# Where the copy of the rotated half into place 4 is written in the row loop of a spectral convolution

## The chip, the core and the metric

The kernel runs on one core of a Trainium2 chip. A core has five engines, each with its own queue of instructions: TensorE (PE in the profile; PEld is its weight load), VectorE (DVE), ScalarE (ACT), GpSimd (POOL) and SyncE (SP), which here only issues DMAs. An engine's sequencer that issues a DMA is shown as SPq or POOLq. The metric is the time of one execution on the device in microseconds (us), the median of the runs shown.

## The reference, cut to what matters

The input is four images of 512 by 512 places with 16 channels, in float32. Two layers follow each other, each added to its input: a convolution with a filter as large as the image, done by Fourier transforms, and a 3 by 3 convolution with a cosine norm. The change lies in the first:

```python
x = x + _L0_conv_ref(_gn(x), h0, numerators, denumerator)
# _L0_conv_ref: the filter is a ratio of two polynomials, H_full in frequency space
X = jnp.fft.rfft2(x, s=(2 * l1, 2 * l2), axes=(-3, -2))
Y = jnp.einsum('...hwi,ijhw->...hwj', X, H_full)
y = jnp.fft.irfft2(Y, s=(2 * l1, 2 * l2), axes=(-3, -2))
return y[..., :l1, :l2, :]
```

`_gn` is a group norm. The einsum mixes the 16 input channels into 16 output channels at every frequency; the changed copy belongs to this step.

## The kernel before, in words

The program has four phases, one after the other: `filter_phase` makes the filter, `forward_phase` transforms the images along their width, `conv_phase` transforms, mixes and transforms back along the height, and `last_phase` finishes the width and does the second layer. The change touches `conv_phase` alone.

`conv_phase` walks over 513 rows. A row is one frequency along the width (the first is done in two planes, which is why there are 513 and not 512). For row n it does the following, spread over five steps of the loop so that several rows are under way at once.

- `load_x` (L697 and on) fetches the row's input and `turn_x` (L708 and on) makes the transform matrix of the row: one ScalarE instruction (tile turn, L718) and one VectorE instruction (L720).
- `x_part` (L723 and on) transforms it with four matrix products into px (L731), and an eviction copies px into **place 0** of the tile xe. The tile xe has eight places; the other seven hold the same spectrum moved by 16 partitions per place, so that `mix` can use them together.
- `x_late` (L738 and on) stores place 0 to the scratch tensor xf_d in device memory (L745). Then GpSimd makes **xl**, place 0 turned by a fixed set of angles, in six instructions: four products into xu (L752), one product into xl (L753) and one sum into xl (L754). Then xl is stored to xf_d as well (L745). The pool of xl has one buffer (`xlp`, one buffer per tile unless another number is given).
- `load_xe` (L766) reads places 1 to 3 and 5 to 7 of xe back from xf_d with two DMAs on SyncE's queue, which move the partitions by their addresses.
- `half_shift` (L760) makes **place 4** without a DMA. Half 0 copies the upper 64 partitions of place 0 into the lower 64 of place 4. Half 1 copies the lower 64 partitions of xl, the rotated half, into the upper 64 of place 4. Both are copies of 64 by 1024 elements on ScalarE (L763). Half 1 is the copy that the change is about.
- `g_part` (L775) expands the row of the filter into gh, `mix` (L792) multiplies xe by gh into pm, and the eviction of pm makes yf. `over_q` (L812) and `over_g` (L842) transform back and store the result to y_d from GpSimd's queue (L868).

Evictions of PSUM go through `evict` (L678 and on): every third is done by VectorE (L681), the others by ScalarE (L683). In nearly every row ScalarE so has 17 instructions: four evictions into yf, four into gh, four copies into zq (L827), one eviction into yo, one into xe, one turn and the two copies of `half_shift`.

What sets the order: `step(n)` (L876) runs for n from -3 to 514 and writes the work in four quarters, k = 0 to 3. Each quarter has a quarter of `mix` of row n, of `g_part` of row n + 1 and of `over_q` of row n - 1. Quarter 0 has also `x_part` and `x_late` of row n + 2, quarter 2 has `turn_x` of row n + 3 and `over_g` of row n - 2. In the kernel before, quarter 2 has half 0 and quarter 3 has half 1 of `half_shift` of row n + 2. No engine's queue is written out by hand: a scheduler takes the instructions in the order of the source as priorities, places each on its engine's queue, and adds the waits that data and buffers demand. Once the program is built, each engine runs its queue in its fixed order.

Of the kernel before, what the change touches and what calls it, by code (L numbers as in the profile page):

```python
# [46 lines left out]
P = 128  # L47
# [153 lines left out]
def bc(ap, axis, shape):  # L201
    return ap.unsqueeze(axis).to_broadcast(shape)
# [447 lines left out]
def conv_phase(tc, cst, g_d, x_d, y_d):  # L650
    nc = tc.nc
    with ExitStack() as ctx:
# [22 lines left out]
        state = {}  # L675
# [9 lines left out]
        def load_g(n):  # L685
            rc, r, plane = rows[n]
            g = io.tile([P, C, 8 * C], F32, name="g")
            t, w = g.rearrange("p j x -> p (j x)"), C * 8 * C
            if plane is None:
                nc.sync.dma_start(out=t, in_=dram(g_d[rc], r, 0, [w, P], [1, w]))  # L690
            else:
                for to, at in ((0, (0, 96)[plane]), (64, (64, 32)[plane])):
                    nc.sync.dma_start(out=t[to : to + 32], in_=dram(g_d[rc], r, at * w, [w, 32], [1, w]))
                    nc.gpsimd.memset(t[to + 32 : to + 64], 0.0)
            state["g", n] = g

        def load_x(n):  # L697
            rc, r, plane = rows[n]
            x = io.tile([P, B, 8 * C], F32, name="x")
            t, w = x.rearrange("p b x -> p (b x)"), B * 8 * C  # L700
            if plane is None:
                nc.sync.dma_start(out=t, in_=dram(x_d[rc], r, 0, [w, P], [1, w]))
            else:
                nc.gpsimd.memset(t[S:], 0.0)
                nc.sync.dma_start(out=t[:S], in_=dram(x_d[rc], r, plane * S * w, [w, S], [1, w]))
            state["x", n] = x

        def turn_x(n):  # L708

            for k in range(2) if n == 0 else [n // 64 + 1] if n % 64 == 0 else []:  # L710
                if k < 9:
                    state["own", k] = xlp.tile([P, 2, 64], F32, name="own", bufs=3)
                    nc.sync.dma_start(
                        out=state["own", k].rearrange("p v n -> p (v n)"), in_=cst["own"][:, 128 * k : 128 * k + 128]
                    )
            own, at = state["own", n // 64], slice(n % 64, n % 64 + 1)
            t = xlp.tile([P, 2 * F], F32, name="turn")
            nc.scalar.activation(t, dfs[:, 1], AF.Identity, scale=own[:, 1, at])  # L718
            m = xlp.tile([P, 2 * F], F32, name="dfs_n", bufs=2)
            nc.vector.scalar_tensor_tensor(m, dfs[:, 0], own[:, 0, at], t, ALU.mult, ALU.add)  # L720
            state["dfs", n] = m

        def x_part(n, b):  # L723

            if b == 0:

                state["xe", n] = xep.tile([P, 8, F, 2, 2, 2], F32, name="xe")
            if b % 2 == 0:
                state["px"] = ps_f.tile([P, 2, F, 2], F32, name="px", tag="full")
            px = state["px"]  # L730
            nc.tensor.matmul(px[:, b % 2].rearrange("p f c -> p (f c)"), state["x", n][:, b],  # L731
                             state["dfs", n], start=True, stop=True)
            if b % 2:
                evict(state["xe", n][:, 0, :, b // 2], px.rearrange("p k f c -> p f c k"))
            if b == B - 1:
                del state["x", n], state["dfs", n]

        def x_late(n):  # L738

            xe = state["xe", n][:, 0]  # L740
            fl = xe.rearrange("p f h c k -> p f (h c k)")

            def store(half, t):
                at = slice(C, P) if half == 0 else slice(0, P - C)
                nc.gpsimd.dma_start(out=xf_d[n % 4][half * P :, :][at], in_=t[at].rearrange("p f x -> p (f x)"))  # L745

            store(0, fl)
            xl = xlp.tile([P, F, 2, 2, 2], F32, name="xl")
            u = xlp.tile([P, F, 2, 2, 2], F32, name="xu")
            for c in range(2):  # L750
                for h in range(2):
                    nc.gpsimd.tensor_mul(u[:, :, h, c], xe[:, :, h, 1 - c], bc(late[:, 1 + c], 2, [P, F, 2]))  # L752
            nc.gpsimd.tensor_mul(xl.rearrange("p f h c k -> p f (h c k)"), fl, bc(late[:, 0], 2, [P, F, 8]))  # L753
            nc.gpsimd.tensor_add(xl.rearrange("p f h c k -> p (f h c k)"),  # L754
                                 xl.rearrange("p f h c k -> p (f h c k)"),
                                 u.rearrange("p f h c k -> p (f h c k)"))
            store(1, xl.rearrange("p f h c k -> p f (h c k)"))
            state["xl"] = xl

        def half_shift(n, half):  # L760

            dst, src = ((slice(0, 64), state["xe", n][64:, 0]), (slice(64, P), state["xl"][:64]))[half]
            nc.scalar.copy(state["xe", n][dst, 4].rearrange("p f h c k -> p (f h c k)"),  # L763
                           src.rearrange("p f h c k -> p (f h c k)"))

        def load_xe(n):  # L766
            src = xf_d[n % 4]
            for t in (1, 5):
                nc.sync.dma_start(
                    out=state["xe", n][:, t : t + 3].rearrange("p t f h c k -> p t (f h c k)"),  # L770
                    in_=bass.AP(tensor=src.tensor, offset=src.offset + t * C * XF,
                                ap=[[XF, P], [C * XF, 3], [1, XF]]),
                )

        def g_part(n, j):  # L775


            if j % 4 == 0:
                state["pg"] = [ps_g.tile([P, 4, F], F32, name=f"pg{c}", tag="pg") for c in range(2)]
            g, pg = state["g", n], state["pg"]  # L780
            for c in range(2):
                half = slice(64 * c, 64 * c + 64)
                nc.tensor.matmul(pg[c][:, j % 4], g[half, j], dg[half], start=True, stop=True)  # L783
            if j == 3:
                state["gh", n] = ghp.tile([P, F, 2, C], F32, name="gh")
            if j % 4 == 3:
                for c in range(2):
                    evict(state["gh", n][:, :, c, j - 3 : j + 1], pg[c].rearrange("p j f -> p f j"))
            if j == C - 1:
                del state["g", n]  # L790

        def mix(n, g):  # L792

            if g % 8 == 0:
                state["pm"] = ps_m.tile([P, 8, 8, 2 * B], F32, name="pm")
            xe, gh, pm = state["xe", n], state["gh", n], state["pm"]
            for q in range(4):
                f = g + 32 * q
                nc.tensor.matmul(  # L799
                    pm[32 * q : 32 * q + 32, g % 8], gh[:, f].rearrange("p c j -> p (c j)"),  # L800
                    xe[:, :, f].rearrange("p t h c k -> p t (h c k)"), start=True, stop=True,
                )
            if g == 7:

                state["y", n] = yp.tile([P, 16, 32, 4], F32, name="yf")
            if g % 8 == 7:
                evict(state["y", n][:, :, g - 7 : g + 1].rearrange("p t g x -> p g t x"),
                      pm.rearrange("p g t (h x) -> p g (t h) x", h=2))
            if g == 31:
                del state["xe", n], state["gh", n]  # L810
# [65 lines left out]
        def step(n):  # L876


            def row(k):
                return 0 <= n + k < n_rows  # L880

            if row(3):
                load_x(n + 3)
            if row(2):
                load_g(n + 2)
            if row(1):
                load_xe(n + 1)
            for k in range(4):
                if row(0):
                    for g in range(8):  # L890
                        mix(n, 8 * k + g)
                if row(1):
                    for j in range(4):
                        g_part(n + 1, 4 * k + j)
                if row(-1):
                    for t in range(4):
                        over_q(n - 1, 4 * k + t)
                if row(2) and k == 0:
                    for m in range(B):
                        x_part(n + 2, m)  # L900
                    x_late(n + 2)
                if row(2) and k >= 2:
                    half_shift(n + 2, k - 2)
                if row(3) and k == 2:
                    turn_x(n + 3)
                if row(-2) and k == 2:
                    for m in range(4):
                        over_g(n - 2, m)

        for n in range(-3, n_rows + 2):  # L910
            step(n)
# [443 lines left out]
```

## Time and profile before

| what | us |
|---|---|
| median of 3 runs | 19007.57 |
| lowest and highest run | 19006.79 and 19023.34 |
| the profiled execution, its own time | 19054.31 |
| its span, first to last instruction | 19052.5 |
| PE busy, DVE busy, ACT busy, POOL busy in the span | 17293.1, 11398.8, 9747.4, 11564.3 |

Instructions of L763 start between 6958.5 us and 16013.2 us of the span, which marks the stretch of `conv_phase`. Over 512 rows, 6966 to 16013 us, a row takes 9047 / 512 = 17.67 us.

How to read a line of the timeline: start, duration, engine, source line, operation, the tile written and the tile read with their sizes, how many instructions are merged, and in brackets how long the engine was idle before it and whose end ended that wait. In a list of waits, the line that waited stands left of the arrow, the line that released it right, then the total, the count and the longest.

### The profile page before, as it was taken

The numbers are of one execution on the slowest core, as the hardware profiler recorded it, in microseconds if no ns is written. First come the engines' busy times: TensorE is split into PE (matmuls) and PEld (weight loads), VectorE is DVE, ScalarE is ACT, GpSimd is POOL, SyncE is SP. The second block draws the span as 40 slices with busy tenths as digits, with TensorE's granted clock in tenths as the row PEclk, the third lists the DMA queues.
The fourth block names the chain that finished last, engine by engine and source line by source line (L and its number), as shares of the span: only waits on it lengthen the run. The fifth ranks groups of instructions, "written<-read, shape, count | busy, mean of one in ns | idle before, by whom it ended". The sixth has DMA issues, their size and how long they took to land. (4 is left out here: it accounts for less than half of the span.)

```text
span 19052.5 us, 536690 instructions
## 1 busy us (share of the span) xinstructions
PE 17293.1 (91%) x227020; PEld 12605.2 (66%) x227020; DVE 11398.8 (60%) x23961; ACT 9747.4 (51%) x17871; POOL 11564.3 (61%) x12445
## 2 busy tenths in 40 slices
PE   8899999999999988898888888888888888979999
PEld 5455555555554457777777777777777776868888
DVE  8877777777763335555555555555555554347656
ACT  4455555555552235555555555555555553107777
POOL 7577777777771126666666666666666664127655
PEclk7899999999999999999999999999999999999999
DMA  3755455555557668888888888888888887796321
GB/s 100 206 153 148 137 150 150 146 139 149 149 151 223 187 211 320 323 322 324 320 322 317 322 327 317 322 324 323 320 325 323 321 320 282 268 321 210 131 72 62
DMA packets 2918658, 4543.39 MB, mean 238 GB/s; under 512 B 117442, under 2 KB 2086300, under 8 KB 2809374
## 3 DMA queue, kind: packets, MB, share of 16 engines
q1 hardware_dynamic: 2686062, 3768.91, 58.5%
q0 software_dynamic: 174896, 605.89, 8.3%
q10 hardware_dynamic: 55296, 134.24, 2.1%
q8 instruction: 1789, 29.31, 0.6%
q14 instruction: 615, 5.04, 0.1%
HBM read 3031.23 MB, written 1477.31 MB: 237 GB/s over the span
## 5 line engine op out<-in xcount | busy, mean ns | idle before, releaser
L783 PE MATMUL pg<-c_dg,g 64*128 64x128 f32 x32832 | 2842.9, 291 | 320.9 <-ACT gh L683 159.5
L799 PE MATMUL pm<-xe,gh 128*32 128x64 f32 x131328 | 2403.4, 222 | 576.2 <-issue 353.1
L799 PEld LDWEIGHTS pm<-xe,gh 128*32 128x32 f32 x131328 | 2012.8, 110 | 1180.2 <-issue 996.4
L783 PEld LDWEIGHTS pg<-c_dg,g 64*128 64x128 f32 x32832 | 2283.2, 190 | 662.7 <-issue 262.5
L372 PE MATMUL pg<-c_dinv,sp 128*128 128x256 f32 x8192 | 2278.4, 426 | 294.3 <-ACT st L377 193.8
L828 DVE TENSOR_TENSOR z<-zq,pz 128x256 f32<-128x256 f32 x2052 | 862.0, 420 | 2617.2 <-ACT zq L827 2534.6
L348 DVE RECIPROCAL dn<-dn 128x256 f32<-128x256 f32 x1024 | 1790.8, 1749 | 778.3 <-POOL dn L341 778.0
L372 PEld LDWEIGHTS pg<-c_dinv,sp 128*128 128x128 f32 x8192 | 1609.9, 207 | 946.8 <-ACT st L377 215.3
L681 DVE COPY gh<-pg 128x512 f32<-128x512 f32 x2046 | 1410.5, 689 | 1294.1 <-PE pg L783 1289.6
L417 PE MATMUL pt<-ev_in,c_todd 128*128 128x512 f32 x4096 | 1970.1, 606 | 45.6 <-DMA ev_in<-g_d 27.0
L752 POOL TENSOR_TENSOR xu<-xe,c_late 128x256 f32<-128x256 f32 x2052 | 1393.4, 705 | 856.3 <-ACT xe L683 832.3
L335 ACT COPY ab<-pab 128x512 f32<-128x512 f32 x2048 | 1104.2, 592 | 1130.1 <-POOL m L355 333.3
L683 ACT COPY yf<-pm 128x512 f32<-128x512 f32 x2046 | 1210.5, 592 | 919.0 <-PE pm L799 904.3
L377 ACT COPY st<-pg 128x256 f32<-128x256 f32 x2048 | 1072.6, 623 | 1024.0 <-PE pg L372 619.3
L763 ACT COPY xe<-xl 64x1024 f32<-64x1024 f32 x513 | 538.8, 1050 | 1877.0 <-POOL xl L754 1877.0
L350 POOL TENSOR_TENSOR x<-ab,ab 128x256 f32<-128x256 f32 x1024 | 875.8, 855 | 933.6 <-ACT ab L335 907.0
L1208 PE MATMUL pc<-l_band,xn 128*128 128x160 f32 (+3 forms) x9024 | 1374.8, 309 | 65.0 <-DVE e_o L1255 64.0
L683 ACT COPY gh<-pg 128x512 f32<-128x512 f32 x2058 | 1201.2, 584 | 402.0 <-PE pg L783 393.6
L820 PE MATMUL pz<-c_ident,yf 128*128 128x128 f32 x8208 | 1378.2, 291 | 27.2 <-issue 25.4
L1208 PEld LDWEIGHTS pc<-l_band,xn 128*128 128x128 f32 x9024 | 1218.8, 197 | 224.7 <-issue 147.2
L329 PEld LDWEIGHTS pab<-c_e,u 18*128 18x128 f32 x8192 | 723.5, 188 | 809.5 <-ACT st L377 452.5
L417 PEld LDWEIGHTS pt<-ev_in,c_todd 128*128 128x128 f32 x4096 | 806.8, 198 | 669.9 <-issue 514.6
(195 smaller groups left out, 33846.4 us busy)
## 6 DMA issues: line engine op xcount, KB each, us to landing
xe<-xf_d SPq DMA_DIRECT2D x1026, 1536.0 KB, 10.3
g<-g_d SPq DMA_DIRECT2D x511, 1024.0 KB, 9.9
g_d<-st SPq DMA_DIRECT2D x64, 4096.0 KB, 34.3
ev_in<-g_d SPq DMA_DIRECT2D x1024, 256.0 KB, 4.8
g_d<-ot SPq DMA_DIRECT2D x1024, 256.0 KB, 2.9
xf_d<-xe POOLq DMA_DIRECT2D x513, 448.0 KB, 8.3
xf_d<-xl POOLq DMA_DIRECT2D x513, 448.0 KB, 5.3
x_d<-xo SPq DMA_DIRECT2D x128, 1024.0 KB, 5.1
```

What stands on the lines that cost most here:

```text
L335: nc.scalar.copy(w["ab"][n], pp[n])
L348: nc.vector.reciprocal(w["dn"], w["dn"])
L372: nc.tensor.matmul(pg[:, k].rearrange("p a x -> p (a x)"), w["sp"][:, k, c, :], dinv[:, 2 * kp + k, c, :], start=(c == 0), stop=(c == 1),)
L377: nc.scalar.copy(st[a][:, :, i].rearrange("p (q k x) -> p k q x", q=2, k=4)[:, 2 * kp : 2 * kp + 2], pg[:, :, a].rearrange("p k (q x) -> p ...
L417: nc.tensor.matmul(pt, todd[:, c, kc, hh * P : hh * P + P], ev[:, kc, c], start=(kc == 0), stop=(kc == 1),)
L681: nc.vector.tensor_copy(dst, src)
L683: nc.scalar.copy(dst, src)
L752: nc.gpsimd.tensor_mul(u[:, :, h, c], xe[:, :, h, 1 - c], bc(late[:, 1 + c], 2, [P, F, 2]))
L783: nc.tensor.matmul(pg[c][:, j % 4], g[half, j], dg[half], start=True, stop=True)
L799: nc.tensor.matmul(pm[32 * q : 32 * q + 32, g % 8], gh[:, f].rearrange("p c j -> p (c j)"), xe[:, :, f].rearrange("p t h c k -> p t (h c k ...
L820: nc.tensor.transpose(pz[:, t % 4].rearrange("p v q x -> p (v q x)"), y[:, at].rearrange("p g x -> p (g x)"), ident)
L1208: nc.tensor.matmul(pc[:, lo:hi, :].rearrange("p w j -> p (w j)"), xns[q][:, h * P + dh : h * P + dh + P], bands[dh][:, o : o + hi - lo, :] ...
```

## The change

Half 1 of `half_shift` is written in quarter 1 of the next step instead of quarter 3 of its own step. It still works on the same row: `half_shift(n + 1, 1)` in step n copies what `x_late` made in step n - 1. As another row's xl has been made in quarter 0 in between, xl is kept in `state` by its row. Half 0 stays in quarter 2.

```diff
             store(1, xl.rearrange("p f h c k -> p f (h c k)"))
-            state["xl"] = xl
+            state["xl", n] = xl
...
-            dst, src = ((slice(0, 64), state["xe", n][64:, 0]), (slice(64, P), state["xl"][:64]))[half]
+            dst, src = ((slice(0, 64), state["xe", n][64:, 0]), (slice(64, P), state["xl", n][:64]))[half]
...
-                if row(2) and k >= 2:
-                    half_shift(n + 2, k - 2)
+                if row(1) and k == 1:
+                    half_shift(n + 1, 1)
+                    del state["xl", n + 1]
+                if row(2) and k == 2:
+                    half_shift(n + 2, 0)
```

## The prediction

> **What bounds the kernel now.** I read the page first: busy shares, then the 40 slices, then the costliest groups. PE is busy for 91% of the span, and in the slices of the row stage its digit is 8 or 9 throughout, while ACT shows 5 and POOL 6. So PE sets the pace of the rows, and ScalarE matters only where PE waits for it. The chain of waits that ended last lies in the last phase and does not bear on the change. The waits of PE in the stretch of the rows, 6966 to 16013 us, say where PE loses time:
>
> ```profile
> PE pm L799 <- issue: 349.6, 355, 3.2
> PE pg L783 <- ACT gh L683: 159.1, 177, 5.4
> PE pg L783 <- issue: 156.6, 111, 3.4
> PE pm L799 <- DMA xe<-xf_d: 73.7, 51, 3.0
> PE pm L799 <- ACT zq L827: 62.3, 172, 0.4
> ```
>
> PE's idle time there, all lines of that list added, is 950 us of 9047. ScalarE's share of it is 159.1 + 62.3 = 221.4 us. The next view is the same list for ScalarE. Its largest wait is the one that the change speaks of:
>
> ```profile
> ACT xe L763 <- POOL xl L754: 1872.7, 512, 6.5
> ```
>
> Once in every row ScalarE stands for 1872.7 / 512 = 3.66 us until GpSimd has the rotated half ready. The timeline of ScalarE shows what stands where in one row:
>
> ```profile
> 10008.87 0.59 ACT L683 COPY xe<-px 128x512 f32<-128x512 f32 x1 [0.45 <-PE px L731]
> 10010.81 1.05 ACT L763 COPY xe<-xe 64x1024 f32<-64x1024 f32 x1 [1.35 <-DVE xe L681]
> 10011.76 0.58 ACT L683 COPY yf<-pm 128x512 f32<-128x512 f32 x1
> 10012.36 0.52 ACT L718 ACTIVATE turn<-c_dfs,own 128x256 f32<-128x256 f32 x1
> 10012.78 0.57 ACT L683 COPY gh<-pg 128x512 f32<-128x512 f32 x1
> 10013.25 0.38 ACT L827 COPY zq<-pz 128x256 f32<-128x256 f32 x1
> 10017.33 1.06 ACT L763 COPY xe<-xl 64x1024 f32<-64x1024 f32 x1 [3.70 <-POOL xl L754]
> 10018.41 0.59 ACT L683 COPY yf<-pm 128x512 f32<-128x512 f32 x1
> ```
>
> The reader is to see two things. The copy of half 1 stands fourth after the copy of half 0, behind the first zq that follows it, and that is quarter 1 of the step. The source before writes half 0 in quarter 2 and half 1 in quarter 3. So the queue is not the order of the source: **the scheduler had already brought both copies (and turn, which the source writes in quarter 2) forward**, to where their inputs are due by its own reckoning. GpSimd's timeline in the same row and the next gives the other end:
>
> ```profile
> 10012.89 1.97 POOL L753 TENSOR_TENSOR xl<-xe,c_late 128x1024 f32<-128x1024 f32 x1
> 10014.94 2.36 POOL L754 TENSOR_TENSOR xl<-xl,xu 128x1024 f32<-128x1024 f32 x1
> 10017.59 0.57 POOL L745 DMA_DIRECT2D xf_d<-xl  x1 [0.29 <-POOL xl L754]
> ...
> 10030.06 1.98 POOL L753 TENSOR_TENSOR xl<-xe,c_late 128x1024 f32<-128x1024 f32 x1
> ```
>
> xl has one buffer. The copy can run between the end of L754 (10017.30) and the next row's L753 (10030.06), which overwrites xl. Any queue that holds the data right must put it in that gap of 12.8 us or hold L753 back.
>
> **The change, part by part.** It adds and removes no instruction: 513 copies of half 1, mean 1049 ns, before and after, the same two store DMAs, the same waits for data. What could change is the place of one instruction in ScalarE's queue, and with it what waits behind it. Whether it changes is a matter of the built programs, because the scheduler, not the source, makes the queues. I laid the two programs' queues beside each other, instruction by instruction. One row of ScalarE's queue, the same places in both (buffer numbers as built, before left of the bar):
>
> ```
> 10017 xe<-px  xe_106040<-px_106041 | xe_106039<-px_106040
> 10018 half 0  xe_106040<-xe_106040 | xe_106039<-xe_106039
> 10019 yf      yf_106012<-pm_106059 | yf_106011<-pm_106058
> 10020 turn                         | the same
> 10021 gh      gh_106024<-pg_106093 | gh_106023<-pg_106092
> 10022 zq      zq_106110<-pz_106105 | zq_106109<-pz_106104
> 10023 half 1  xe_106040<-xl_106050 | xe_106039<-xl_106049
> ```
>
> In both, half 1 copies the xl of the row whose place 0 was evicted six instructions earlier. The buffer numbers are smaller by one because the source makes its names one copy earlier; the row is the same. The source now writes the copy half a step later, and the scheduler brings it forward by that much more, to the same place. Over the whole program the queues have the same lengths (ScalarE 24,789 entries with its pure waits, GpSimd 16,634, VectorE 27,854, TensorE 122,696, SyncE 9,324), and place by place the same operations, shapes, buffer addresses and waits with the same counts. What differs is names and line numbers.
>
> So the sum is: instructions added 0, removed 0, moved 0; DMAs moved on SyncE's or GpSimd's queue 0; the stall of 3.66 us in each row stays; **change 0 us**. The profiled execution, 19054.31 us with a span of 19052.5, lies 46.7 us above the median of the three runs; a sum of zero on it is a sum of zero on the median, and the forecast is the median, 19007.57 us.
>
> The Trainium skill has a rule that such a stall invites: "Perfetto Trace Analysis", section Optimization Strategy, says that a gap that repeats on the engine that ought to be saturated can come from too few buffers for the next tile. The row against it: in the rows' stretch GpSimd never waits for the copy before it overwrites the single xl (its L753 waited 3.1 us in all, and for a DMA), and the engine with the gap is not the saturated one. By the rule a later copy would need a second buffer before it could pay; by the row the buffer is not what holds ScalarE. Neither moves the sum, as no instruction moves.
>
> **The rivals.**
>
> 1. *The move does reach the queue and frees ScalarE (faster).* This is what the words of the change say. Then the 3.66 us stall goes and the evictions behind it come on time. Speaking for it: the stall is in 512 rows, and in the row after the one shown PE stood 1.10 us for an eviction of gh just after it. Against it: the two queues above. What it would give: nothing, where the yf and gh evictions are early enough; at most all of PE's idle time, 950 us; I take ScalarE's part of PE's waits, 221.4 us, since the other releasers are not ScalarE's: 19007.57 - 221.4 = 18786 us.
>
> 2. *The move reaches the queue and holds GpSimd back (slower).* With one buffer of xl, the next row's L753 must wait for the copy. In the next row zq of quarter 1 begins at 10030.39 and takes 0.38, the copy 1.05 behind it would end at 10031.82, and L753, which began at 10030.06, would begin 1.76 us late. The sum L754 and the store behind it on GpSimd's queue come as late, then the loads of xe on SyncE's queue, and mix at the end. It decides from the point where the loads of xe are what PE waits for, which they are already in 51 rows (73.7 us). GpSimd itself idles enough to hide it (2.38 us before its next store to y_d in that row). If none is absorbed, 512 x 1.76 = 901 us: 19909 us. If all is, 0. Against it again the queues.
>
> 3. *The same program, but its time lies elsewhere than the three runs (either way).* The three runs span 16.5 us, 0.09%. A difference of more than 0.2%, 38 us, which is about what a measurement of this kernel can tell from no change, would be over twice that.
>
> **How the numbers follow.** The forecast, no change, gets 0.96. Rival 1 gets 0.01 and rival 2 gets 0.01, since both need a queue other than the one built. Rival 3 gets 0.02, one half to each side. So faster 0.02, same 0.96, slower 0.02. The time is the median, 19007.57 us. For the range no unknown cost is left, only the scatter of the runs: the lowest run less their whole spread, 19006.79 - 16.5 = 18990, and the highest plus it, 19023.34 + 16.5 = 19040. Cases outside it hold less than 2 in 10.
>
> **What would show it.** In the profile of the changed kernel ScalarE should wait for GpSimd's xl 512 times or so, about 1870 us in all, now under the same line number. The timeline should have half 1 behind turn, gh and zq, and L753 should wait for nothing of ScalarE's. PE's wait for ScalarE's gh should be near 160 us. It would be wrong if the wait for xl were gone or much shorter, if L753 (with its line as it is) waited for the copy, or if the copies of half 1 began a row later than their xl ended. A span that differs by more than 38 us with all these rows alike would speak for rival 3.

## The result, and the profile after

The changed kernel took 19012.21 us, the median of 12 runs from 18977.92 to 19042.25 us. Beside it the kernel before took 19014.25 us, the median of 12 runs from 18987.79 to 19045.35 us. The ratio is 1.0 with a 95% interval from 0.9993 to 1.0008: no difference that can be measured. The profiled execution of after has a span of 19024.1 us against 19052.5 us before, which is within the scatter of the runs.

The rows that the prediction rests on, in the profile after. First PE's waits in the rows' stretch (6966 to 16013 us); the columns are total us, times, longest:

```profile
PE pm L799 <- issue: 312.7, 320, 2.9
PE pg L783 <- ACT gh L683: 182.3, 197, 5.1
PE pg L783 <- issue: 149.5, 102, 3.2
PE pm L799 <- DMA xe<-xf_d: 95.0, 62, 3.0
PE pm L799 <- ACT zq L827: 63.5, 178, 0.4
```

ScalarE's waits in the same stretch:

```profile
ACT xe L763 <- POOL xl L754: 1881.9, 513, 6.5
```

The stall is where it was: 1881.9 us in 513 rows, 3.67 us each, against 1872.7 us in 512 rows before. PE's rows differ by up to 37 us with no change of order, which says how far one profiled execution of this kernel is to be read. ScalarE's timeline in one row, and then GpSimd's:

```profile
10014.84 0.59 ACT L683 COPY xe<-px 128x512 f32<-128x512 f32 x1 [0.45 <-PE px L731]
10016.91 1.04 ACT L763 COPY xe<-xe 64x1024 f32<-64x1024 f32 x1 [1.48 <-DVE xe L681]
10017.86 0.57 ACT L683 COPY yf<-pm 128x512 f32<-128x512 f32 x1
10018.46 0.51 ACT L718 ACTIVATE turn<-c_dfs,own 128x256 f32<-128x256 f32 x1
10018.88 0.57 ACT L683 COPY gh<-pg 128x512 f32<-128x512 f32 x1
10019.45 0.38 ACT L827 COPY zq<-pz 128x256 f32<-128x256 f32 x1
10023.47 1.05 ACT L763 COPY xe<-xl 64x1024 f32<-64x1024 f32 x1 [3.63 <-POOL xl L754]
```

```profile
10021.07 2.36 POOL L754 TENSOR_TENSOR xl<-xl,xu 128x1024 f32<-128x1024 f32 x1
10023.73 0.58 POOL L745 DMA_DIRECT2D xf_d<-xl  x1 [0.29 <-POOL xl L754]
...
10035.90 1.97 POOL L753 TENSOR_TENSOR xl<-xe,c_late 128x1024 f32<-128x1024 f32 x1
```

Half 1 still stands behind yf, turn, gh and zq, the fifth instruction after half 0 (the prediction's "fourth" is a miscount of the same rows); it starts 0.04 us after the sum L754 of its own row has ended (10021.07 + 2.36 = 10023.43), and the next L753 waits for nothing. The copy that the source now writes in the next step runs where it always ran. Over the whole program the two traces have, engine by engine, the same operations on the same tiles in the same order: 17,871 instructions on ScalarE, 12,445 on GpSimd, 23,961 on VectorE. Of TensorE's 227,020 matmuls 8 stand in other places, all of them products into py that change places with a neighbour in the record.

### The profile page after: what moved, and what is told of

Read it like the earlier page. It is cut to its first block, busy times and chain, and to the rows that moved or that the text cites. A ratio compares the mean times of both kernels' runs of the same rounds, so it can differ in the third digit from the quotient of the medians.

```text
span 19024.1 us, 536690 instructions
## 1 busy us (share of the span) xinstructions
PE 17301.1 (91%) x227020; PEld 12607.2 (66%) x227020; DVE 11386.2 (60%) x23961; ACT 9742.6 (51%) x17871; POOL 11567.4 (61%) x12445
## 5 line engine op out<-in xcount | busy, mean ns | idle before, releaser
L763 ACT COPY xe<-xl 64x1024 f32<-64x1024 f32 x513 | 538.6, 1050 | 1881.9 <-POOL xl L754 1881.9
```

## The experiments

The change never reached the queue, so its result says nothing of what the words describe. The experiments make the move real and then ask why it is worth what it is worth. In these kernels `state["zq"]` holds the last zq copy that was written, and `tc.issue_after(ins)` adds an edge of the issue order: what is written under it stands behind `ins` in that engine's queue. It adds no wait for data. "Before" is the kernel before, run beside each group on the same chip. Its median moved between groups (19015.5 to 19071.95 us), so each version is given as a ratio to the runs of "before" in its own group.

| what | ratio to before, 95% interval |
|---|---|
| half 1 reads place 0: no stall | 1.0008, 0.9999 to 1.0017 |
| half 1 behind quarter 2 | 1.0, 0.9991 to 1.0009 |
| half 1 behind quarter 3 | 1.0004, 0.9995 to 1.0014 |
| half 1 behind quarter 1 of the next step, one xl | 1.0047, 1.0034 to 1.006 |
| the same, two xl | 1.0017, 1.0009 to 1.0026 |
| half 1 behind quarter 3, half of xu on VectorE | 0.9996, 0.9987 to 1.0004 |
| half the filters not loaded, stall kept | 1.0009, 1.0 to 1.0018 |
| half the filters not loaded, half 1 behind quarter 3 | 0.982, 0.9807 to 0.9833 |
| half the filters not loaded, half 1 in the next step | 0.9858, 0.9842 to 0.9875 |
| place 2 by copies on both engines, half 1 behind quarter 3 | 1.1662, 1.1646 to 1.1678 |
| place 2 by copies on both engines, stall kept | 1.1497, 1.1481 to 1.1514 |
| place 2 by copies on ScalarE, half 1 behind quarter 3 | 0.9907, 0.9893 to 0.992 |

**The stall alone.** Half 1 reads place 0, which is ready long before.

```diff
-... (slice(64, P), state["xl"][:64]))[half]
+... (slice(64, P), state["xe", n][:64, 0]))[half]
```

> Half 1 of half_shift reads place 0 (the evicted spectrum) instead of xl, so the upper half of place 4 isn't the rotated half and the product is another; the copy keeps its shape, its length and about its place, but waits for GpSimd no longer. It prices the stall of 3.66 us per row alone. Theory A (the stall costs what PE waits for ScalarE behind it): PE's 159 us for gh and 62 us for zq mostly go, 100 to 220 us faster, 18790 to 18910 us. Theory B (the stall is hidden, because the evictions wait out in PSUM buffers and PE's row is set by its own work and by the loads of xe): within 0.2% of before, under 38 us. Both expect ScalarE's wait for xl at zero.

Measured: 1.0008, so the end of the stall alone wins nothing. Its 3.66 us per row went, and with it PE's waits for ScalarE's gh and zq (zq: 0.7 us; no row for gh); PE's wait for the loads of xe took their place (253.0 us in 128 waits, against 73.7 before):

```profile
PE pm L799 <- DMA xe<-xf_d: 253.0, 128, 4.9
```

The copy was expected to keep about its place and didn't: the two copies now have only a yf between them and stand ahead of turn, gh and zq. Theory B holds for the time. Theory A was right that PE's waits for ScalarE go, and wrong that the time goes with them.

**The move made real, in three steps.**

```diff
-                if row(2) and k >= 2:
-                    half_shift(n + 2, k - 2)
+                if row(2) and k == 2:
+                    half_shift(n + 2, 0)
+                if row(2) and k == 3:        # 2 in the first version
+                    with tc.issue_after(state["zq"]) if "zq" in state else ExitStack():
+                        half_shift(n + 2, 1)
```

In the third version the last two lines stand ahead of half 0, with `row(1) and k == 1` and `half_shift(n + 1, 1)`.

> Half 1 really moves: an edge in the issue order holds it behind the zq copy of quarter 2 of the same step, three instructions later in ScalarE's queue; one buffer of xl. The evictions of yf, gh and zq that stood behind the stall now stand ahead of it. Theory A: the wait for xl falls from 3.66 us per row to 1 us or less and PE's waits for ScalarE fall by more than half, 100 to 200 us faster. Theory B: same within 38 us. A move that harms (the eviction into yo now stands behind the copy, as does the rest) would show as slower by over 38 us.

> As the one before, but half 1 is held behind the zq copy of quarter 3, seven instructions later, about where the source before writes it. Theory A: the wait for xl is gone (xl is ready some 4 us earlier), 100 to 220 us faster. Theory B: same within 38 us. L753 of the next row starts some 9 us later, so it should not wait for the copy under either.

> Half 1 is held behind the zq copy of quarter 1 of the next step, 16 instructions later: what the words of the change say, with one buffer of xl, as the changed source has it. The second rival of the prediction: L753 of the next row waits for the copy, 1.76 us per row late at the timings of before, so GpSimd shows a wait for ScalarE's L763-line copy in nearly every row, and the time is up to 901 us longer if nothing absorbs it. Theory A with GpSimd's idle time absorbing it: 100 to 220 us faster. Theory B: same. I expect the wait to be there and most of it absorbed: between 100 us faster and 200 us slower.

Measured: 1.0, 1.0004 and 1.0047. Behind quarter 3 ScalarE's wait for xl is gone, and the list of PE's waits is another:

```profile
PE pm L799 <- issue: 423.7, 399, 4.3
PE pm L799 <- DMA xe<-xf_d: 295.9, 122, 4.9
PE pg L783 <- issue: 148.7, 117, 3.2
...
PE pg L783 <- ACT gh L683: 11.5, 3, 5.8
```

Against before, the wait for ScalarE's gh fell from 159.1 to 11.5 us and the wait for the loads of xe rose from 73.7 to 295.9 us. What ScalarE gave back, the loads took; the row of mix without a releaser rose as well, from 349.6 to 423.7 us. The granted clock was a little lower, 0.97 against 0.98 between 7000 and 15600 us, but PE's busy time per matmul was 43.9 ns in both (7663.80 us over 174516 matmuls, 7699.59 over 175214 before), so the clock isn't what took the gain. Behind quarter 2 part of ScalarE's wait stays, 543.0 us in 370 waits, and PE's wait for gh is down to 11.0 us all the same.

In the next step, with one buffer of xl, GpSimd's timeline has the wait that the prediction's second rival worked out:

```profile
10014.04 1.97 POOL L753 TENSOR_TENSOR xl<-xe,c_late 128x1024 f32<-128x1024 f32 x1 [1.82 <-ACT xe L763]
10016.09 2.38 POOL L754 TENSOR_TENSOR xl<-xl,xu 128x1024 f32<-128x1024 f32 x1
```

L753 stands 1.82 us for the copy in this row and 907.8 us in all. Yet the kernel lost only 0.47%, some 90 us (0.0047 x 19058). PE's largest wait is now the loads of xe, 428.1 us in 230 waits. My expectation of the wait and of its absorption held; theory A's gain did not come.

**Is L753's wait the cost?** Two buffers of xl; xu moves to place 5 of xe to make room.

```diff
-            xl = xlp.tile([P, F, 2, 2, 2], F32, name="xl")
-            u = xlp.tile([P, F, 2, 2, 2], F32, name="xu")
+            xl = xlp.tile([P, F, 2, 2, 2], F32, name="xl", bufs=2)
+            u = state["xe", n][:, 5]
```

> Half 1 forced to quarter 1 of the next step again, but with two buffers of xl, so that L753 need not wait for the copy; to make room xu is kept in place 5 of the same row's xe, which the load fills only later. If the 0.47% that the one-buffer version lost came from L753's wait (908 us in its profile) through the later store and loads, this one is the same as before within 0.2%, and GpSimd's wait for the copy and the added wait of PE for the loads of xe are gone. If it came from the later copy itself or from something else in that order, it stays 0.3 to 0.6% slower.

Measured: 1.0017. L753's wait is gone here, and the loss is 0.17% instead of 0.47%. The two ratios come from two groups and xu has moved as well, so that L753's wait made up most of the loss is likely and not cleanly shown. The remainder of 0.17% is just clear of zero; whether it is the later copy or the other place of xu wasn't tried apart. One part of the expectation failed: PE's added wait for the loads of xe isn't gone. It is 275.2 us up to 15900 us, near the 295.9 of half 1 behind quarter 3.

**What the loads are worth, with the stall and without.**

```diff
             rc, r, plane = rows[n]
+            if n > 3 and n % 2:
+                state["g", n] = state["g", n - 1]
+                return
             g = io.tile([P, C, 8 * C], F32, name="g")
```

> The kernel before with every second row's filter left out: odd rows reuse the tile g of the row before, so 1024 KB less are loaded in every second row (9% of the 5504 KB that a row moves); the result uses the wrong filter there. The stall of ScalarE stays. Theory C (the rows are paced by how many bytes the DMA engines can move, 0.87 busy at 321 GB/s): PE's waits for the loads of xe go and the time falls, by at most 9% of 9047 = 840 us, by 150 us or more. Theory D (they are paced by the chain from GpSimd's xl through its store to the load, whatever the bytes): less than 80 us. Theory E (PE's own work paces them): within 38 us.

> The same with every second row's filter left out, and with half 1 held behind the zq copy of quarter 3, so without ScalarE's stall. If the stall was worth nothing only because the loads set the pace, it is worth something here: 60 to 220 us faster than the version that leaves out the filter alone. If the stall is hidden by PE's own work too, the two are within 38 us of each other.

> Every second row's filter left out, and half 1 held behind the zq copy of quarter 1 of the next step with one buffer of xl: what the words of the change say, where the loads have room. Theory F: ScalarE's stall is gone and the loads have slack to take up L753's wait of some 1.8 us, 200 to 350 us faster. If L753's wait and the later store cost time even then: within 100 us of before or slower.

Measured: 1.0009, 0.982 and 0.9858. The first two, beside half 1 behind quarter 3 (1.0004), settle the cause. Taking the stall away gives nothing, making the loads lighter gives nothing, and both together give 1.8%. Theory C fails by itself, since the lighter loads alone won nothing. Theories D and E foresaw just that and fail in the second version: it differs from half 1 behind quarter 3 (1.0004) in the loads of the filter alone, neither in GpSimd's instructions nor in PE's, and is 362.5 us faster than the one with the stall (19077.4 to 18714.86 us). That is more than the 60 to 220 us expected. PE's waits with lighter loads and the stall kept (three lines added to the function, so mix is L802 and gh's product L786):

```profile
PE pm L802 <- issue: 539.4, 453, 4.0
PE pg L786 <- issue: 139.4, 105, 4.3
PE pg L786 <- ACT gh L683: 121.6, 136, 5.1
PE pm L802 <- ACT zq L830: 108.2, 293, 0.6
```

The loads of xe are in no row of the list any more; ScalarE's gh and zq are, 229.8 us. The row of mix without a releaser rose from 349.6 to 539.4 us. With the stall gone as well:

```profile
PE pm L802 <- issue: 498.8, 417, 4.3
PE pg L786 <- issue: 155.7, 132, 3.1
...
PE pg L786 <- ACT gh L683: 10.6, 3, 5.1
...
PE pm L802 <- DMA xe<-xf_d: 7.3, 11, 3.1
```

The waits for ScalarE and for the loads are near zero, and only then do the rows come faster. The version in the next step gains 1.4% with lighter loads although L753 still waits (937.4 us up to 15900 us): the move that the words of the change describe would have paid where the loads have room.

**Bytes or the chain to the load?** Two of the four products into xu on VectorE shorten GpSimd's chain.

```diff
-                    nc.gpsimd.tensor_mul(u[:, :, h, c], ...)
+                    (nc.vector if c else nc.gpsimd).tensor_mul(u[:, :, h, c], ...)
```

> Half 1 held behind the zq copy of quarter 3, and two of the four products into xu are made by VectorE instead of GpSimd, so that GpSimd's chain to the rotated half is 1.4 us shorter per row and its store leaves earlier; the bytes are the same. Theory D: PE's wait for the loads of xe (296 us with half 1 in quarter 3) falls by half or more and the time by 100 to 250 us. Theory C: it falls little, the time is within 60 us of before, as VectorE has the time to spare.

Measured: 0.9996, and PE's wait for the loads of xe 276.1 us up to 15900 us, hardly less than the 295.9 up to 16013. The result is not a clean one: the store of place 0 now waited for VectorE (780.4 us in all on GpSimd) and PE again waited for gh (110.1 us). It speaks for the bytes, against the chain, but doesn't decide it alone.

**A version that takes both away.** Place 2 of xe is place 0 moved by 32 partitions. It can be copied on the core in four pieces, which saves 512 KB of 5504 KB per row.

```diff
+        def quarter_shift(n, q):
+            xe = state["xe", n]
+            src = xe[32 * q + 32 : 32 * q + 64, 0] if q < 3 else state["xl", n][:32]
+            (nc.vector.tensor_copy if q < 2 else nc.scalar.copy)(
+                xe[32 * q : 32 * q + 32, 2].rearrange("p f h c k -> p (f h c k)"),
+                src.rearrange("p f h c k -> p (f h c k)"))
...
-            for t in (1, 5):
+            for t, m in ((1, 1), (3, 1), (5, 3)):
```

> A version with the right result that lightens the loads as well as taking ScalarE's stall away: place 2 of xe, which is place 0 moved by 32 partitions, is made by four copies of 32 by 1024 elements (two on VectorE, two on ScalarE) instead of being loaded, 512 KB of a row's 5504 KB; half 1 and the copy of xl for place 2 stand behind the zq copy of quarter 3. Theory F (the stall and the loads pace the rows side by side, so that both must go): PE's wait for the loads goes and the time falls as with every second filter left out, 200 to 350 us, if the four copies (about 1 us each) hide in the idle time of their engines. If the copies crowd ScalarE's and VectorE's evictions: less than 100 us, or slower, with PE waiting for ACT or DVE.

> Place 2 made by the four copies, but half 1 left where the scheduler puts it, so that ScalarE still stalls for xl once per row. Theory F: most of the gain of the version before is missing, within 80 us of the kernel before. If the loads alone were the bound: as fast as the version with half 1 behind quarter 3, within 60 us.

Measured: 1.1662 and 1.1497. The copies crowd VectorE's evictions, the branch that was expected if they don't hide, but by far more than expected, and theory F was not tested by these two. VectorE's two copies are the reason, as PE's largest wait and lines of the timeline show, VectorE's with GpSimd's work beside it (quarter 3 version, the wait from 6966 to 15900 us):

```profile
PE pg L790 <- DVE gh L681: 1842.2, 368, 5.8
...
9004.69 7.02 DVE L769 COPY xe<-xe 32x1024 f32<-32x1024 f32 x2
9005.14 1.36 POOL L752 TENSOR_TENSOR xu<-xe,c_late 128x256 f32<-128x256 f32 x2
9006.47 1.96 POOL L753 TENSOR_TENSOR xl<-xe,c_late 128x1024 f32<-128x1024 f32 x1
9008.50 2.67 POOL L754 TENSOR_TENSOR xl<-xl,xu 128x1024 f32<-128x1024 f32 x1
9011.75 0.69 DVE L681 COPY gh<-pg 128x512 f32<-128x512 f32 x1
9012.49 0.58 PE L790 MATMUL pg<-c_dg,g 64*128 64x128 f32 x2 [5.47 <-DVE gh L681]
```

Two copies take 7.02 us, over GpSimd's whole chain, the eviction of gh stands behind them, and PE stands 5.47 us for that eviction. Waiting isn't the whole loss: between 7000 and 15600 us PE was busy 51.3 ns per matmul (6629.49 us over 129222) against 43.9 before. So all four copies went to ScalarE, spread over the quarters:

```diff
-            (nc.vector.tensor_copy if q < 2 else nc.scalar.copy)(
+            nc.scalar.copy(
...
+                if row(2) and 1 <= k <= 2:
+                    with tc.issue_after(state["zq"]) if "zq" in state else ExitStack():
+                        for q in ((0,), (1, 2))[k - 1]:
+                            quarter_shift(n + 2, q)
```

> The version with place 2 made by copies once more, with all four copies on ScalarE, where one took 1.05 us (on VectorE 3.44 us beside GpSimd's work), and spread: one behind the zq copy of quarter 1, two behind that of quarter 2, and the one of xl behind half 1 after quarter 3. Theory F, with the copies hidden in ScalarE's idle time: 150 to 350 us faster than before, PE's wait for the loads of xe gone. If 4.2 us more on ScalarE, in pieces of 1 to 2 us ahead of evictions, cost PE as much as the loads did: within 80 us of before, with PE waiting for ACT. Slower by more than 100 us would mean that ScalarE has become the bound.

Measured: 18835.22 us against 19015.5 us, 0.9907. It is faster than the kernel before by 0.93% (0.80 to 1.07%), with the full computation. ScalarE works 6717.11 us of the 8600 us from 7000 to 15600, against 4538.22 before, and PE's list of waits has no row for the loads of xe any more. PE's first waits there:

```profile
PE pm L806 <- issue: 420.2, 357, 4.2
PE pg L790 <- DMA g<-g_d: 126.8, 102, 5.7
```

What is late next is the load of the filter, 126.8 us in 102 waits.

## Why the prediction was right, point by point

- **The sum of zero.** The step that carried it was to compare the queues that the two sources become, and not the sources. It held: the trace after has the same order on every engine (but for the 8 records named above) and the same place of half 1, the same stall (1881.9 against 1872.7 us) and the same time, 1.0. The forecast needed no reading of what the stall is worth, and that reading, in rival 1, would have failed.
- **Why the place is the same.** I put it down to the scheduler, which places the copy where its input is due. One run speaks for that: where half 1 reads place 0, which is ready earlier, the copy stands three instructions further ahead, though no line was moved in the source. Otherwise it took an edge of the issue order to move it. Whether the one buffer of xl has a part in its place, no run here shows.
- **Rival 1, faster by 221 us.** Its chance was small because the queue doesn't change, and that was right. Its price was wrong, though: with the stall truly gone the gain is 0 (1.0008, 1.0, 1.0004), not 221 us. I read PE's waits for ScalarE as time to be won. They were time that the loads of xe would have taken in any case; the row of 73.7 us for those loads in the profile before was the second bound, seen where the first one happened to end earlier. Where the stall's end does pay, with lighter loads, it pays more than that list says: 362.5 us, with 229.8 us of PE's waits for gh and zq before it.
- **Rival 2, slower by up to 901 us.** The mechanism and its size per row were right: 1.76 us foreseen, 1.82 us seen; 901 us foreseen, 907.8 us of waiting seen. What came out at the end was some 90 us, a tenth. The absorption, whose size I left open, took the rest.
- **The rule on buffers** (the Trainium skill, "Perfetto Trace Analysis", section Optimization Strategy). For the kernel as it stands the row won: after the change too L753 waits 3.2 us in all, and for a DMA, so there is no wait for a second buffer to take away. Where the copy does move a row later, L753 waits 907.8 us for it, and the version with a second buffer (and xu moved) loses 0.17% instead of 0.47%. The rule points that way, though the gap there is on GpSimd and not on the engine that ought to be saturated, of which the rule speaks.
- **The scatter.** I took the three runs' spread, 16.5 us, for the kernel's. Twelve runs of the kernel before spread over 57.6 us (18987.79 to 19045.35), 0.30%. The median lay within the range, but three of the twelve runs after the change didn't (18977.92, 18982.26 and 19042.25 us), and in three of the four later groups the median of the kernel before was above it (19057.81, 19061.97 and 19071.95 us). That so narrow a range held is luck in part.

What stays open: PE's waits with no releaser in the profile ("issue"), the largest of them at mix (349.6 us before, 539.4 with lighter loads): the trace shows only that nearly all of these begin inside a run of 64 matmuls, where no other engine is waited for; the remaining 0.17% with two buffers; and whether the loads are limited by bytes or by latency, for which lighter loads (0.80 instead of 0.87 busy) and the fewer bytes of the last version, in one load more per row, speak; no run kept the bytes and cut the latency cleanly.

## What to carry to other kernels

Where a scheduler makes the queues, read the built queues before the profile: a line moved in the source may move nothing. A stall that repeats in every row, and even the waits of the busiest engine that end with it, is worth only the distance to the next bound; look in the same list for who would be late next, and take two bounds of like size away together before judging either. A change that gives nothing alone is not thereby useless.

## What the runs showed of the hardware that was not expected

- A copy of 32 by 1024 elements from SBUF to SBUF on VectorE took very different times in one and the same kernel (place 2 on both engines, half 1 behind quarter 3). The first line gives the shortest, the middle and the longest of the 1026 copies in ns, the second a pair of them that had none of GpSimd's arithmetic beside it:

```profile
L769 DVE COPY xe<-xe x1026: 680/2734/4307, 6959.4 to 19194.8; 32x1024 f32<-32x1024 f32 x171
7745.12 1.38 DVE L769 COPY xe<-xe 32x1024 f32<-32x1024 f32 x2
```

The 19 copies that overlap none of GpSimd's arithmetic took 0.68 us each, and all others 0.89 to 4.31 us; the mean of the 722 up to 15600 us is 3.44 us. So it is GpSimd's work beside them that makes them long. GpSimd's L754 took 2670 ns there against 2358 ns before, and the same copy on ScalarE took 1.05 us. The Trainium skill, "SBUF — State Buffer", section Terms, says that VectorE and GpSimd share a pair of SBUF ports which one holds for a whole instruction while the other is blocked. The longer times on both engines agree with it; that the ports are the reason is the page's statement and not shown by a run.
- ScalarE's copy takes 1.05 us for 32 partitions by 1024 elements and for 64 by 1024 alike: half the partitions didn't make it shorter.
- The granted clock was lower where PE was busy less: 0.98 with PE busy for 7699.59 of 8600 us (before, 7000 to 15600 us), 0.84 with PE busy for 6629.49 of 8600 us (place 2 on both engines, half 1 behind quarter 3). PE's busy time per matmul was 51.3 ns there and 43.9 before. With 360 matmuls in a row and 512 rows, this is an estimated 1.4 of the 3.2 ms lost, the rest being PE's idle time; how much of it the clock alone makes was not taken apart.
